# The first right factor of the hyperbolic layer is made under the decay layer, its first products get other PSUM banks, and the row-end products move behind them

## The chip, the cores and the metric

One core of one Trainium2 chip runs the kernel. The metric is the device time of one launch in microseconds, as a median over repeated executions. One more execution is taken by the hardware profiler; all rows and times of day (us from the start of the span) come from that one.

## What is computed

Four graph layers run one after the other on a node matrix x (4096 x 64) and one dense adjacency matrix adj (4096 x 4096, fp32, symmetric pattern but not symmetric values, all entries at least 0). Every layer ends in `x = layernorm(x + layer(x, adj))`. Cut to what matters here:

```python
# layer 0: Chebyshev filter, K = 4: x, L@x, 2L(L@x)-x, ... each times its weight
# layer 1: gated cell and signed attention over adj
# layer 2, "decay": only the last 100 neighbours of a row count, weight halves per step
support = input @ weight
mask = (adj != 0); rank = cumsum(mask, axis=1); deg = rank[:, -1:]
k = minimum(deg, 100); pos = rank - (deg - k)
w = mask * where(pos > 0, 0.5 ** (k - pos), 0.0)
out = w @ support + bias
# layer 3, "hyperbolic": all pairs of nodes
w = adj / adj.sum(axis=1)
log_ij = logmap(x[:, None, :], x[None, :, :])          # mobius_add, norm, arctanh for every pair
agg = einsum('ij,ijc->ic', w, log_ij)
out = expmap(0, agg @ weight + bias)
```

## The kernel before, in words

The nodes are cut into 32 blocks of 128 (NB), eight groups of four blocks (NG, GB = 4, so a group is 512 nodes, GW). The program is written with a tile framework: it allots SBUF and PSUM from pools that open and close as scopes, orders the instructions of each engine by its own priorities, and sets the semaphores. Where `in_order(...)` stands around an instruction, that instruction keeps the written order against the others so marked. PSUM has eight banks of 128 x 512 fp32, and pools take them from bank 0 upwards in the order in which they are opened.

**Layer 2 (lines 1399 to 1512).** The groups are done in two turns, first groups 4 to 7, then 0 to 3. In a turn the loop goes over 64 half blocks h from the last to the first. For each, TensorE adds the masks to the counts (`cnt_ps`, L1450: four products with the constant `follow` into two banks), ScalarE turns the first bank into weights (`wt`, L1455), and VectorE the second (L1457), or ScalarE both while there are seam steps to do (`busy`). One block later TensorE gathers with these weights into four banks `acc_ps` (L1410, L1422). At the end of a turn `copies` (L1479, VectorE) takes the four banks to SBUF as `decayed[g]`.

What follows on a turn is cut into small steps in the list `seam`, of which the loop does one per block: `ends(two)` (L1343) takes two groups through the row-end products with the weight `wd` (`summed`, L1360, eight products, and L1364 on VectorE), the layernorm and the preparation for layer 3 (`turn_prepared`, L1288: transposes into `tr_c` and `tr_o`). The seam of turn 0 is done under turn 1, and the seam of turn 1 under the beginning of layer 3. At the very beginning of layer 2 the seam holds the end of layer 1's last group: edge products (L937, L944), a tanh with a table load (L953), and so on; there ScalarE also copies the last two banks of layer 1 (L1462, L1463), after which these banks go to `acc_ps`.

The pools of layer 2 are opened in the order `ps_c2` (counts: banks 0 and 1), `ps_p2` (two `post` banks: 2 and 3), and then `ps_a2` (the four `acc_ps`: 4 to 7).

**Layer 3 (from line 1514).** It opens `ps_v3` (two buffers of two banks: 0 to 3), `ps_a3` (4 and 5) and `ps_p3` (`post`, 6 and 7). The pairs of nodes are a triangle of 36 tiles of 512 x 512 (`tiles`), rows in the order 4, 5, 6, 7, 0, 1, 2, 3 (`seq`); each is done in two units, n = 0 to 71. A unit n goes through

- `product(n)` (L1577, fp32, four passes of TensorE) of `tr_c` with the right factor of the row, `rights[i][0]`,
- `square(n)` (L1586, ScalarE), then `opposite(n)` (L1596, TensorE, bf16, onto the same banks) with the second right factor,
- `less_one(n)` (L1604, VectorE), a logarithm and two exponentials on ScalarE (L1801, L1802, L1828), the sum with the products (L1826, VectorE), which gives the banks of `product(n)` back to `product(n + 2)`, one more logarithm (L1837),
- `f` (L1811) and `at_d` (L1814) on VectorE, then, a unit later, `gather` (L1638, L1650) on TensorE, and `turn` (L1622 and L1624) for the mirrored half of the tile.

`right(i)` (L1525) makes the right factors of a row: four fp32 and four bf16 products into two `post` banks (L1531) and two copies on ScalarE (L1534) to `rv` and `ro`. For the first row it is called just ahead of `product(0)`; for the others three tiles before they are needed. What a row gathers lies in the two halves of a bank `sums_ps`: partitions 0 to 63 take `at_d`, 64 to 127 take `at_m`. The mirrored sums of a column are kept from row to row in the lower half of `tb`, and for each tile off the diagonal below the first row they are put back by one product with a part of the identity, L1646. That product reads all 128 partitions of `tb`, so its upper half is filled with zeros at the start of the layer (L1544, seven memsets on VectorE).

The beginning of layer 3 is written so:

```python
rights[seq[0]] = right(seq[0])
product(0)
square(0)
less_one(0)
opposite(0)
product(1)
```

Of the kernel before, what the change touches and what calls it, by code (L numbers as in the profile page):

```python
# [28 lines left out]
V_FLOOR = 2.0**-21  # L29
# [33 lines left out]
def gnn4_kernel(  # L63
# [813 lines left out]


    turns_of = [list(range(NG - QG, NG)), list(range(NG - QG))]

    def load2(to, groups, c):

# [456 lines left out]


    decayed = {}

    def ends(two):  # L1343

        bs = slice(two[0] * GB, (two[1] + 1) * GB)
        x2 = nat_a[:, bs, 0:F]
        small = {
            name: sm.tile([P, 2 * GB], F32, name=name) for name in ("ln_ve", "ln_s", "ln_r")
        }
        ve, s, r = small["ln_ve"], small["ln_s"], small["ln_r"]  # L1350
        mv = sm.tile([P, 2 * GB, 2], F32, name="ln_mv")

        def over_all(t):
            return t.unsqueeze(2).to_broadcast([P, 2 * GB, F])

        def summed(ps_p):
            o = ps_p.tile([P, GB, 2 * F], F32, name="post", tag="post")
            for b in range(GB):
                for q, g in enumerate(two):
                    nc.tensor.matmul(  # L1360
                        o[:, b, q * F : (q + 1) * F], lhsT=decayed[g][:, cols(b)], rhs=wd, start=True, stop=True
                    )
            halves = "p (q b) f -> p q b f"
            nc.vector.tensor_tensor(  # L1364
                x2.rearrange(halves, q=2), o.rearrange("p b (q f) -> p q b f", q=2),
                nat_b[:, bs, :].rearrange(halves, q=2), ALU.add,
            )
            st = sm.tile([P, 2 * GB, 6], F32, name="ln_st")
            for b in range(2 * GB):
                nc.vector.bn_stats(st[:, b, :], x2[:, b, :])  # L1370
                nc.vector.bn_aggr(mv[:, b, :], st[:, b, :])
            nc.vector.tensor_scalar_add(ve, mv[:, :, 1], LN_EPS)

        def roots(ps_p):
            nc.scalar.activation(s, ve, AF.Ln)
            nc.scalar.activation(s, s, AF.Exp, scale=0.5)

        def rest(ps_p):

            nc.vector.reciprocal(r, s)  # L1380
            nc.vector.tensor_tensor(r, ve, r, ALU.mult)
            nc.vector.tensor_tensor(s, s, r, ALU.add)
            nc.vector.reciprocal(r, s)
            nc.vector.tensor_scalar_mul(r, r, 2.0)
            nc.vector.tensor_tensor(x2, x2, over_all(mv[:, :, 0]), ALU.subtract)
            nc.vector.tensor_tensor(x2, x2, over_all(r), ALU.mult)

            nc.vector.scalar_tensor_tensor(s, mv[:, :, 1], float(F), r, ALU.mult, ALU.mult)
            nc.vector.tensor_tensor(n2[:, bs], s, r, ALU.mult)

            nc.vector.tensor_reduce(ve, x2, AX.X, ALU.add)
            nc.vector.tensor_scalar_mul(ve, ve, 1.0 / F)
            nc.vector.tensor_tensor(x2, x2, over_all(ve), ALU.subtract)

        return [summed, roots, rest, lambda ps_p: prepare(two)] + [
            lambda ps_p, g=g: turn_prepared(ps_p, g) for g in two
        ]

    with tc.tile_pool(name="mask2", bufs=3) as mk_p, tc.tile_pool(name="wt2", bufs=3) as wt_p, tc.tile_pool(
        name="ps_c2", bufs=1, space=PSUM  # L1400
    ) as ps_c, tc.tile_pool(name="ps_p2", bufs=2, space=PSUM) as ps_p, ExitStack() as ps_a_open:

        def masks2():
            return [mk_p.tile([P, CB, GW], MASK, name=f"m{n}") for n in range(2 * QG)]
# [26 lines left out]
        for turn, groups in enumerate(turns_of):  # L1431
# [9 lines left out]
            for h in reversed(range(2 * NB)):  # L1441
# [31 lines left out]

                gathers += lo + two if jb == 0 else two + lo
                if jb == 0:
                    def copies(ps_p, acc=acc, groups=groups):
                        for q, g in enumerate(groups):
                            decayed[g] = three.tile([P, GW], F32, name=f"sums{q}")
                            nc.vector.tensor_copy(decayed[g], acc[q])  # L1479

                    assert turn == 0 or not seam
                    seam += [lambda ps_p: None, copies]
                    for a in range(2):
                        seam += ends((groups[2 * a], groups[2 * a + 1]))
                busy = bool(seam)
                if seam:
                    seam.pop(0)(ps_p)
# [18 lines left out]

    with tc.tile_pool(name="o3", bufs=1) as op, tc.tile_pool(name="cols3", bufs=3) as cols_p, tc.tile_pool(
        name="w3", bufs=4  # L1510
    ) as wp3, tc.tile_pool(name="el3", bufs=3) as el, tc.tile_pool(name="f3", bufs=2) as fp, tc.tile_pool(
        name="r3", bufs=2
    ) as rp, tc.tile_pool(name="ps_v3", bufs=2, space=PSUM) as ps_v, tc.tile_pool(
        name="ps_a3", bufs=2, space=PSUM
    ) as ps_a, tc.tile_pool(name="ps_p3", bufs=2, space=PSUM) as ps_p:
        HB = CB // 2

        tb = op.tile([P, N], F32, name="tb")
# [1 line left out]
        spread_w = two_w[:, F : 2 * F]  # L1520
        kappa = op.tile([P, 2, NB], F32, name="kappa")

        rvs = [op.tile([P, GW], F32, name=f"rv{q}") for q in range(2)]
        ros = [op.tile([P, GW], BF16, name=f"ro{q}") for q in range(2)]

        def right(i):
            q = seq.index(i) % 2
            for to, w, t in ((rvs[q], to_right, tr_c), (ros[q], to_other, tr_o)):
                ps = ps_p.tile([P, GW], F32, name="post", tag="post")
                for b in range(GB):  # L1530
                    nc.tensor.matmul(  # L1531
                        ps[:, cols(b)], lhsT=w[:, b % 2, :], rhs=t[:, (i * GB + b) // 2, :], start=True, stop=True
                    )
                nc.scalar.copy(to, ps)  # L1534
            return rvs[q], ros[q]


        seq = turns_of[0] + turns_of[1]
        tiles = [(i, j) for n, i in enumerate(seq) for j in seq[n:]]
        NT = len(tiles)  # L1540
        own, mirrored = {}, {}
        nc.gpsimd.memset(tb[F:P, gcols(seq[0])], 0.0)
        for g in seq[1:]:
            nc.vector.memset(tb[0:F, gcols(g)], 0.0)  # L1544

        def load_own(t):
            if t < NT and t not in own:
# [12 lines left out]
            i, j = tiles[n // 2]  # L1560
            return slice(2 * P if i == j and n % 2 else 0, GW)

        rights, sums, fs = {}, {}, {}
        vs, ws, rts = {}, {}, {}
        NU = 2 * NT

        def product(n):

            if n >= NU:
                return  # L1570
            i, j = tiles[n // 2]
            vs[n] = ps_v.tile([P, HB, GW], F32, name="v_ps")
            cs = columns(n)
            for k in range(HB):
                jb = j * CB + (n % 2) * HB + k
                half = slice(jb % 2 * F, jb % 2 * F + F)
                in_order(nc.tensor.matmul(  # L1577
                    vs[n][:, k, cs], lhsT=tr_c[half, jb // 2, :], rhs=rights[i][0][half, cs], start=True, stop=True
                ))

        def square(n):
            if n >= NU:
# [5 lines left out]
        def opposite(n):  # L1588
            if n >= NU:
                return  # L1590
            i, j = tiles[n // 2]
            cs = columns(n)
            for k in range(HB):
                jb = j * CB + (n % 2) * HB + k
                half = slice(jb % 2 * F, jb % 2 * F + F)
                in_order(nc.tensor.matmul(  # L1596
                    vs[n][:, k, cs], lhsT=tr_o[half, jb // 2, :], rhs=rights[i][1][half, cs],
                    start=False, stop=True, skip_group_check=True,
                ))

        def less_one(n):
            if n < NU:
                w = ws[n][:, :, columns(n)]
                nc.vector.tensor_scalar(w, w, -SCALE * SCALE, V_FLOOR * (V_FLOOR + 2.0) * SCALE**2, ALU.add, ALU.max)  # L1604

        def turn(n):

# [19 lines left out]
        def gather(t, h, tm):  # L1627
# [8 lines left out]
            for k in (HB * h, HB * h + 1):  # L1636
                if t is not None:
                    in_order(nc.tensor.matmul(  # L1638
                        bank[0:F, :], lhsT=nat_c[:, j * CB + k, :], rhs=own[t][:, k, :],
                        start=(i == j and k == 0), stop=(j == seq[-1] and k == CB - 1), skip_group_check=True,  # L1640
                    ))
                if tm is not None:
                    above, below = tiles[tm]
                    if k == 0 and above != seq[0]:

                        in_order(nc.tensor.matmul(  # L1646
                            bank[F:P, :], lhsT=ident[:, F:P], rhs=tb[:, gcols(below)],
                            start=True, stop=False, skip_group_check=True,
                        ))
                    in_order(nc.tensor.matmul(  # L1650
                        bank[F:P, :], lhsT=nat_c[:, above * GB + k, :], rhs=mirrored[tm][:, k, :],
                        start=(k == 0 and above == seq[0]), stop=(k == CB - 1), skip_group_check=True,
                    ))
# [125 lines left out]
        for t in range(3):  # L1779
            load_own(t)  # L1780
            load_mirrored(t)
        rights[seq[0]] = right(seq[0])
        product(0)
        square(0)
        less_one(0)
        opposite(0)
        product(1)
        n = 0
        while n < NU + 2 or turns or gathers:
            if n % 2:  # L1790
# [51 lines left out]
                    seam.pop(0)(ps_p)  # L1842
            if n + 6 < NU and tiles[(n + 6) // 2][0] not in rights:
                i = tiles[(n + 6) // 2][0]
                rights[i] = right(i)
            n += 1

        before, last = seam[:-6], seam[-5:]
# [49 lines left out]
```

## Time and profile before

| what | us |
|---|---|
| median of three executions (1404.11, 1404.13, 1407.46) | 1404.13 |
| the profiled execution | 1408.86 |
| its span, first to last instruction | 1407.1 |
| layer 2, from the first counts to the last gather | 762.8 to 964.2 |
| layer 3 and the end of layer 2, from there on | 964.2 to 1407.1 |
| TensorE busy over the span | 1310.2 (93%) |
| VectorE busy | 1052.1 (75%) |
| ScalarE busy | 805.7 (57%) |

A row of the timeline has the start, the duration, the engine (PE is TensorE's multiplication, PEld its weight load, DVE VectorE, ACT ScalarE, POOL GpSimd), the line, the operation, what it writes and reads with its tile shape, and in brackets the idle time of the engine just before it and what ended that. An fp32 product is two passes in the rows. A row of the table by stages has the busy time of each engine in a stretch, and behind them the granted clock of TensorE (1.00 is full), the share of the DMA engines and GB/s.

### The profile page before, as it was taken

The page shows a single profiled execution, that of the slowest core. Times are in us where ns is not written, and L with a number is a line of the kernel's source. Part 1 is how long each engine was busy: PE and PEld are TensorE (multiplying, and loading weights), DVE is VectorE, ACT ScalarE, POOL GpSimd, SP SyncE. Part 2 cuts the span into 40 slices and gives each one's busy share as a digit, 9 for nine tenths or more (in the row PEclk, how much of TensorE's full clock was granted, in tenths as well). Part 3 has the DMA queues.
Part 4 walks back from the last instruction along what each step waited for, and adds up shares of the span by engine and source line. Part 5 has one row for each costly group of instructions (what it writes and reads, how often), then busy time and mean ns, then how long its engine had stood idle before and what let it go on. Part 6 is the DMA issues. An engine that isn't in the chain of part 4 may idle for free.

```text
span 1407.1 us, 19039 instructions
## 1 busy us (share of the span) xinstructions
PE 1310.2 (93%) x6790; PEld 611.1 (43%) x6790; DVE 1052.1 (75%) x2015; ACT 805.7 (57%) x1341; POOL 110.5 (8%) x191
## 2 busy tenths in 40 slices
PE   7999999999999999999999999997889898989893
PEld 5655556556544334444444323333333333333341
DVE  7599889999434257788885224356999999999997
ACT  4544434434000115654424675744989999999894
POOL 2111111011123000010111000000000000000000
PEclk9999999999999999999999999997999999999998
DMA  9999999999799999999985755534244354445330
GB/s 317 392 390 412 376 410 400 405 404 384 290 381 372 388 419 373 421 350 340 329 306 179 239 173 165 181 120 180 78 162 187 149 229 158 184 154 198 138 120 12
DMA packets 108191, 382.16 MB, mean 272 GB/s; under 512 B 20276, under 2 KB 20280, under 8 KB 76472
## 3 DMA queue, kind: packets, MB, share of 16 engines
q1 hardware_dynamic: 87096, 296.17, 57.0%
q0 software_dynamic: 12736, 76.29, 13.2%
q10 hardware_dynamic: 8256, 8.39, 1.7%
q8 instruction: 56, 0.92, 0.3%
q14 instruction: 47, 0.39, 0.1%
HBM read 294.05 MB, written 85.20 MB: 270 GB/s over the span
## 4 chain that ended last, share of the span: by engine, by line
PE 59%; ACT 15%; DVE 15%; DMA 6%; issue 3%; SPq 1%; ACTq 0%; POOL 0%; DVEq 0%
PE pass L566 7%; PE tp L723 6%; PE w_ps L566 6%; PE pass L559 4%; PE cnt_ps L1450 4%; PE a_last L1181 4%; PE a_ps L1181 4%; PE acc_ps L1410 3%; DMA raw<-in_adj_dram 3%; PE h_ps L559 3%; ACT w L1801 2%; ACT rt L1802 2%; DVE rt L1826 2%; ACT w L1586 2%; DVE at_m L1624 2%
## 5 line engine op out<-in xcount | busy, mean ns | idle before, releaser
L730 ACT COPY at<-tp 128x512 f32<-128x512 f32 x248 | 128.5, 598 | 124.2 <-issue 88.6
L1455 ACT ACTIVATE wt<-cnt_ps 128x512 uint16<-128x512 f32 x210 | 116.5, 595 | 65.3 <-PE cnt_ps L1450 63.0
L758 DVE TENSOR_REDUCE dpart<-raw 128x4 f32<-128x2048 f32 x64 | 145.4, 2274 | 4.8 <-DMA raw<-in_adj_dram 4.7
L1638 PE MATMUL sums_ps<-at_d,some 128*64 128x512 f32 x288 | 144.3, 621 | 2.7 <-DVE at_d L1617 1.7
L760 DVE TENSOR_REDUCE lows<-raw 128x1 f32<-128x2048 f32 x64 | 145.4, 2272 | 0.0
L723 PE MATMUL tp<-ident,raw 128*128 128x128 f32 x1024 | 134.4, 285 | 9.8 <-DMA raw<-in_adj_dram 8.3
L723 PEld LDWEIGHTS tp<-ident,raw 128*128 128x128 f32 x1024 | 117.8, 146 | 46.8 <-issue 37.3
L1650 PE MATMUL sums_ps<-at_m,some 128*64 128x512 f32 x224 | 110.0, 613 | 0.0
L1577 PE MATMUL v_ps<-rv,tr_a 64*128 64x512 f32 (+1 forms) x288 | 82.6, 652 | 21.1 <-DVE rt L1826 20.8
L566 PE MATMUL pass<-at,cheb_n 128*128 128x512 f32 x224 | 97.5, 593 | 0.5 <-DVE cheb_n L792 0.5
L566 PE MATMUL w_ps<-at,cheb_n 128*128 128x512 f32 x200 | 91.8, 602 | 0.0
L1826 DVE SCALAR_TENSOR_TENSOR rt<-v_ps,rt 128x1024 f32<-128x1024 f32 x72 | 83.2, 1156 | 5.3 <-ACT rt L1802 4.7
L1450 PE MATMUL cnt_ps<-m,follow 128*64 128x512 fp8e4 x480 | 81.7, 391 | 4.6 <-ACT wt L1455 1.5
L1814 DVE TENSOR_TENSOR at_d<-at_d,f 128x1024 f32<-128x1024 f32 x72 | 83.2, 1156 | 0.1
L1811 DVE SCALAR_TENSOR_TENSOR f<-rt,w 128x1024 f32<-128x1024 f32 x72 | 83.1, 1158 | 0.2 <-ACT rt L1837 0.2
L1624 DVE TENSOR_TENSOR at_m<-post,at_m 128x512 f32<-128x512 f32 x112 | 74.9, 680 | 8.6 <-PE post L1622 8.4
L1837 ACT ACTIVATE rt<-rt 128x1024 f32<-128x1024 f32 x72 | 72.1, 1005 | 11.4 <-DVE rt L1826 10.8
L1457 DVE TENSOR_SCALAR wt<-cnt_ps 128x512 uint16<-128x512 f32 x46 | 31.8, 692 | 59.0 <-PE cnt_ps L1450 59.0
L1801 ACT ACTIVATE w<-w 128x1024 f32<-128x1024 f32 x72 | 72.0, 1000 | 6.5 <-DVE w L1604 6.4
L1622 PE MATMUL post<-ident,f 128*128 128x128 f32 x448 | 68.9, 284 | 4.8 <-DVE at_m L1624 4.5
L1828 ACT ACTIVATE w<-w 128x1024 f32<-128x1024 f32 x72 | 72.4, 1006 | 0.6
L1802 ACT ACTIVATE rt<-w 128x1024 f32<-128x1024 f32 x72 | 72.4, 1005 | 0.6
(426 smaller groups left out, 2279.7 us busy)
## 6 DMA issues: line engine op xcount, KB each, us to landing
at<-adj_t SPq DMA_DIRECT2D x119, 1024.0 KB, 8.5
raw<-in_adj_dram SPq DMA_DIRECT2D x64, 1024.0 KB, 13.3
adj_t<-at POOLq DMA_DIRECT2D x62, 1024.0 KB, 8.2
at_d<-adj_t SPq DMA_DIRECT2D x36, 1024.0 KB, 4.6
at_m<-adj_t SPq DMA_DIRECT2D x28, 1024.0 KB, 6.7
m<-mask_t SPq DMA_DIRECT2D x120, 128.0 KB, 2.9
m<-mask_t SPq DMA_DIRECT2D x60, 256.0 KB, 4.2
mask_t<-mask ACTq DMA_DIRECT2D x28, 256.0 KB, 7.5
```

The source lines that it names most:

```text
L566: in_order(nc.tensor.matmul(ps, lhsT=cheb_n[:, jb, k : k + 2, :], rhs=rhs, start=first, stop=last))
L723: in_order(nc.tensor.transpose(tp[:, cols(b)], raw[:, b, cols(k)], ident))
L730: nc.scalar.copy(at[:, k, :], tp)
L758: in_order(nc.vector.tensor_reduce(dpart[:, g, c, :], raw, AX.X, ALU.add))
L760: in_order(nc.vector.tensor_reduce(lows[:, n : n + 1], raw.rearrange("p b j -> p (b j)"), AX.X, ALU.min))
L1181: in_order(nc.tensor.matmul(ps[q * F : (q + 1) * F, :], lhsT=nat_a[:, c * CB + k, 0:F], rhs=of[q if signed else 0][:, k, :], start=(c == 0 ...
L1450: in_order(nc.tensor.matmul(cnt[a][r * HP : (r + 1) * HP, :], lhsT=follow, rhs=chunks[c][odd][2 * a + r][:, k, :], start=(h == 2 * NB - 1) ...
L1455: in_order(nc.scalar.activation(wt[odd][a], cnt[a], AF.Relu, scale=-128.0))
L1624: work.append(lambda to=to, tp=tp: nc.vector.tensor_tensor(to, tp, to, ALU.mult))
L1638: in_order(nc.tensor.matmul(bank[0:F, :], lhsT=nat_c[:, j * CB + k, :], rhs=own[t][:, k, :], start=(i == j and k == 0), stop=(j == seq[-1] ...
L1650: in_order(nc.tensor.matmul(bank[F:P, :], lhsT=nat_c[:, above * GB + k, :], rhs=mirrored[tm][:, k, :], start=(k == 0 and above == seq[0]), ...
L1826: nc.vector.scalar_tensor_tensor(rt, vs[n][:, :, cs], (1.0 + V_FLOOR) * SCALE, rt, ALU.max, ALU.add)
```

## The change

- `right` is moved up into layer 2. For the first row it becomes the last step of turn 0's seam, so it is done under turn 1. The factors no longer have tiles of their own: the two `rv` lie in an unused quarter of `some`, the first `ro` in `wq_signed`, which layer 1 has left; the second `ro` stays a tile.
- `ps_p2` is opened ahead of `ps_c2`, and `ps_p3` ahead of `ps_v3` and `ps_a3`. So `post` gets banks 0 and 1 in both layers, the counts 2 and 3, and in layer 3 the first product buffer gets 2 and 3, the second 4 and 5, and `sums_ps` 6 and 7.
- Of the four copies at the end of turn 1 two go to ScalarE.
- `product(1)` is written ahead of `less_one(0)` and `opposite(0)`, and from the first product on `behind` chains instructions by ordering them without a semaphore: on TensorE products 0 and 1, `opposite(0)` and then the row-end products, on VectorE `less_one(0)` and then the first sum of the row ends.
- L1646 reads the lower 64 partitions of `tb` alone, with a 64 x 64 part of the identity; the memsets of the upper half go.

```diff
+    rights, begun = {}, {}
+    rvs = [some[:, N // 4 + q * GW : N // 4 + (q + 1) * GW] for q in range(2)]
+    ros = [wq_signed.rearrange("p q h -> p (q h)")[:, 0 : GW // 2].bitcast(BF16)]
+
+    def behind(engine, ins):
+
+        if engine in begun:
+            tc.add_manual_dep(
+                ins.ins, begun[engine],
+                mybir.DependencyInfo(mybir.DependencyClass.NoSync, mybir.DependencyReason.DATA),
+                reason="behind",
+            )
+        begun[engine] = ins.ins.name
...
     with tc.tile_pool(name="mask2", bufs=3) as mk_p, tc.tile_pool(name="wt2", bufs=3) as wt_p, tc.tile_pool(
-        name="ps_c2", bufs=1, space=PSUM
-    ) as ps_c, tc.tile_pool(name="ps_p2", bufs=2, space=PSUM) as ps_p, ExitStack() as ps_a_open:
+        name="ps_p2", bufs=2, space=PSUM
+    ) as ps_p, tc.tile_pool(name="ps_c2", bufs=1, space=PSUM) as ps_c, ExitStack() as ps_a_open:
...
-                    def copies(ps_p, acc=acc, groups=groups):
+                    def copies(ps_p, acc=acc, groups=groups, turn=turn):
                         for q, g in enumerate(groups):
                             decayed[g] = three.tile([P, GW], F32, name=f"sums{q}")
-                            nc.vector.tensor_copy(decayed[g], acc[q])
+                            copy = nc.scalar.copy if turn and q > 1 else nc.vector.tensor_copy
+                            copy(decayed[g], acc[q])
...
                         seam += ends((groups[2 * a], groups[2 * a + 1]))
+                    if turn == 0:
+                        seam.append(lambda ps_p: right(ps_p, seq[0]))
...
-    with tc.tile_pool(name="o3", bufs=1) as op, tc.tile_pool(name="cols3", bufs=3) as cols_p, tc.tile_pool(
+    with tc.tile_pool(name="ps_p3", bufs=2, space=PSUM) as ps_p, tc.tile_pool(name="o3", bufs=1) as op, tc.tile_pool(name="cols3", bufs=3) as cols_p, tc.tile_pool(
...
-        for g in seq[1:]:
-            nc.vector.memset(tb[0:F, gcols(g)], 0.0)
...
-                            bank[F:P, :], lhsT=ident[:, F:P], rhs=tb[:, gcols(below)],
+                            bank[F:P, :], lhsT=ident[F:P, F:P], rhs=tb[F:P, gcols(below)],
...
-        rights[seq[0]] = right(seq[0])
         product(0)
         square(0)
+        product(1)
         less_one(0)
         opposite(0)
-        product(1)
```

More of the change, by code (lines that the diff above doesn't have):

```diff
@@ L879, in gnn4_kernel @@
     turns_of = [list(range(NG - QG, NG)), list(range(NG - QG))]
+    seq = turns_of[0] + turns_of[1]
     def load2(to, groups, c):
@@ L1341, in gnn4_kernel, with right @@
     decayed = {}
+    rights, begun = {}, {}
+    rvs = [some[:, N // 4 + q * GW : N // 4 + (q + 1) * GW] for q in range(2)]
+    ros = [wq_signed.rearrange("p q h -> p (q h)")[:, 0 : GW // 2].bitcast(BF16)]
+    def right(ps_p, i):
+        q = seq.index(i) % 2
+        for to, w, t in ((rvs[q], to_right, tr_c), (ros[q], to_other, tr_o)):
+            ps = ps_p.tile([P, GW], F32, name="post", tag="post")
+            for b in range(GB):
+                nc.tensor.matmul(
+                    ps[:, cols(b)], lhsT=w[:, b % 2, :], rhs=t[:, (i * GB + b) // 2, :], start=True, stop=True
+                )
+            nc.scalar.copy(to, ps)
+        rights[i] = rvs[q], ros[q]
+    def behind(engine, ins):
[4 more added lines that the diff above has]
+                reason="behind",
+            )
+        begun[engine] = ins.ins.name
     def ends(two):
@@ L1359, in summed @@
                 for q, g in enumerate(two):
-                    nc.tensor.matmul(
+                    ins = nc.tensor.matmul(
                         o[:, b, q * F : (q + 1) * F], lhsT=decayed[g][:, cols(b)], rhs=wd, start=True, stop=True
                     )
+                    if begun:
+                        behind("PE", ins)
             halves = "p (q b) f -> p q b f"
-            nc.vector.tensor_tensor(
+            ins = nc.vector.tensor_tensor(
                 x2.rearrange(halves, q=2), o.rearrange("p b (q f) -> p q b f", q=2),
@@ L1367, in summed @@
             )
+            if begun:
+                behind("DVE", ins)
             st = sm.tile([P, 2 * GB, 6], F32, name="ln_st")
@@ L1514, in gnn4_kernel @@
         name="ps_a3", bufs=2, space=PSUM
-    ) as ps_a, tc.tile_pool(name="ps_p3", bufs=2, space=PSUM) as ps_p:
+    ) as ps_a:
         HB = CB // 2
@@ L1521, in gnn4_kernel @@
         kappa = op.tile([P, 2, NB], F32, name="kappa")
[L1523 to L1538, printed above, removed]
         tiles = [(i, j) for n, i in enumerate(seq) for j in seq[n:]]
@@ L1561, in columns @@
             return slice(2 * P if i == j and n % 2 else 0, GW)
-        rights, sums, fs = {}, {}, {}
+        sums, fs = {}, {}
+        ros.append(op.tile([P, GW], BF16, name="ro1"))
         vs, ws, rts = {}, {}, {}
@@ L1576, in product @@
                 half = slice(jb % 2 * F, jb % 2 * F + F)
-                in_order(nc.tensor.matmul(
+                ins = nc.tensor.matmul(
                     vs[n][:, k, cs], lhsT=tr_c[half, jb // 2, :], rhs=rights[i][0][half, cs], start=True, stop=True
-                ))
+                )
+                in_order(ins)
+                if n < 2:
+                    behind("PE", ins)
         def square(n):
@@ L1595, in opposite @@
                 half = slice(jb % 2 * F, jb % 2 * F + F)
-                in_order(nc.tensor.matmul(
+                ins = nc.tensor.matmul(
                     vs[n][:, k, cs], lhsT=tr_o[half, jb // 2, :], rhs=rights[i][1][half, cs],
                     start=False, stop=True, skip_group_check=True,
-                ))
+                )
+                in_order(ins)
+                if n < 1:
+                    behind("PE", ins)
         def less_one(n):
@@ L1603, in less_one @@
                 w = ws[n][:, :, columns(n)]
-                nc.vector.tensor_scalar(w, w, -SCALE * SCALE, V_FLOOR * (V_FLOOR + 2.0) * SCALE**2, ALU.add, ALU.max)
+                ins = nc.vector.tensor_scalar(
+                    w, w, -SCALE * SCALE, V_FLOOR * (V_FLOOR + 2.0) * SCALE**2, ALU.add, ALU.max
+                )
+                if n < 1:
+                    behind("DVE", ins)
         def turn(n):
@@ L1844, in gnn4_kernel @@
                 i = tiles[(n + 6) // 2][0]
-                rights[i] = right(i)
+                right(ps_p, i)
             n += 1
```

## The prediction

> **What bounds the kernel now.** I read the page's sums first, then the table by stages, the chain of waits from 900 to 1010 us, and the timeline row by row at the three places that the edits touch.
>
> ```profile
> PE 1310.2 (93%) x6790; PEld 611.1 (43%) x6790; DVE 1052.1 (75%) x2015; ACT 805.7 (57%) x1341; POOL 110.5 (8%) x191
> ```
>
> TensorE leads, but the sum mixes stages. The table (stretch, length, then PE, PEld, DVE, ACT, POOL; granted clock; DMA share; GB/s) separates them:
>
> ```profile
> 900.00:925.00 25.00, 24.75 (x218) 8.15 (x215) 9.77 (x26) 15.20 (x29) 0.62 (x2) 1.00 0.54 171
> 964.00:975.00 11.00, 8.31 (x40) 6.06 (x39) 6.79 (x14) 2.10 (x3) 0.52 (x1) 0.66 0.89 362
> 975.00:990.00 15.00, 9.17 (x27) 2.62 (x23) 14.53 (x49) 13.53 (x18) 0.00 (x0) 0.50 0.38 156
> 990.00:1010.00 20.00, 18.97 (x80) 7.96 (x80) 19.30 (x40) 19.09 (x22) 0.80 (x2) 0.96 0.28 105
> 1100.00:1200.00 100.00, 90.59 (x429) 36.59 (x428) 96.41 (x155) 96.29 (x132) 1.56 (x2) 1.00 0.45 171
> ```
>
> In layer 2 (first row) TensorE has no gap: each microsecond added there is paid. At the seam (second row) nobody is full, so a chain of waits decides. From 975 VectorE is the bound (14.53 of 15, 19.30 of 20), and later VectorE and ScalarE (96 of 100) with TensorE at 90.6. The seam's chain, by rows of the timeline:
>
> ```profile
> 963.97 2.48 DVE L1479 COPY sums<-acc_ps 128x512 f32<-128x512 f32 x4 [1.24 <-PE acc_ps L1410]
> 966.51 1.16 PE L1531 MATMUL post<-tr_a,to_right 128*128 128x128 f32 x8 [2.36 <-DVE sums L1479]
> 967.75 0.59 ACT L1534 COPY rv<-post 128x512 f32<-128x512 f32 x1 [5.27 <-PE post L1531]
> 968.39 2.08 PE L1577 MATMUL v_ps<-rv,tr_a 64*128 64x512 f32 x4 [0.33 <-ACT rv L1534]
> 970.39 3.67 PE L1360 MATMUL post<-wd,sums 128*128 128x64 f32 x16
> 970.56 1.02 ACT L1586 ACTIVATE w<-v_ps 128x1024 f32<-128x1024 f32 x1 [1.74 <-PE v_ps L1577]
> ...
> 974.10 0.69 DVE L1364 TENSOR_TENSOR nat_a<-post,tr_a 128x512 f32<-128x512 f32 x1 [3.83 <-PE post L1360]
> 974.71 0.68 DVE L1604 TENSOR_SCALAR w<-w 128x1024 f32<-128x1024 f32 x1
> ```
>
> Four copies, right factors, their copy, product(0), row ends, and only then VectorE's run from 974.10. The granted clock is 1.00 up to 967, 0.79 in 967 to 968 and 0.50 until about 991.7, so the row ends take 3.67 us here; the same 16 passes took 2.00 at 893.21 and at 1000.00.
>
> **Part 1: `right` under the decay layer.** It now stands between a gather and a count at about 913, where TensorE has no gap. Its passes at full clock are the rows of a later row: 8 fp32 in 1.13 (1034.51 to 1035.64) and 4 bf16 in 0.32 (1036.71 to 1037.03), 1.45 us. The loop gets one more step with `busy` set; such a step of layer 2 took 2.89 us against 2.72, +0.17 at most. Its two copies (0.59 each) join ScalarE's queue, with both weight pieces of that block behind them and TensorE behind those; ScalarE has 10 us idle in 25, so I take nothing, at worst 0.33. Sum **+1.6** (1.45 to 1.95). It issues no DMA. The seven memsets (L1544) that go took 3.73 us at 966.50, all inside VectorE's 3.83 us wait ahead of 974.10, so their going is worth 0.
>
> **Part 2: the beginning of layer 2.** The built order shows a move that the diff does not: with `ps_p2` in the counts' old banks, ScalarE does weights 1, copy `last_p`, weights 2, the table load (1.28), both tanh (0.28 each), copy `last_a`, and only then weights 3 and 4. Before, both copies stood ahead, and the second tanh came behind weights 3 and 4:
>
> ```profile
> 763.27 1.09 ACT L1455 ACTIVATE wt<-cnt_ps 128x512 uint16<-128x512 f32 x2
> 764.24 0.59 ACT L1463 COPY last_a<-a_last 128x512 f32<-128x512 f32 x1
> 764.71 1.12 ACT L1455 ACTIVATE wt<-cnt_ps 128x512 uint16<-128x512 f32 x2
> 765.84 1.28 ACT L953 ACT_TABLE_LOAD   x1
> 767.14 0.28 ACT L953 ACTIVATE rz<-post 128x128 f32<-128x128 f32 x1
> ```
>
> The second tanh needs the second set of edge products, which ends at 767.8 (L944, 767.30 + 0.49). Then tanh to 768.1, `last_a` to 768.65, two weights to 769.7: the third counts, at 767.73 today, come at about 769.65, and the first gather (behind `last_a`, which frees its banks) at 770.5 instead of 768.28: +2.2. A later wait of TensorE for a mask transfer (0.60 at 779.54) swallows part, since the transfer does not move. **+1.6** (0 if a second such wait does the same, 2.2 if none).
>
> **Part 3: entry of layer 3.** The counts' banks have had their last reader before the last gather. But in the built program the first matmul of product(0) waits for all four `sums` copies: the new pools wait for the old ones as a whole. The copies, two on each engine, end near 963.97 + 2 x 0.62 = 965.3 instead of 966.45. Product(0) then starts at about 965.35 (968.39 today), at full clock lasts 1.13 (L1577, 1035.64), Square 1.02 from 966.55, product(1) beside it, opposite(0) at 967.6, row ends at about 968.0, and L1364's successor at 968.0 + 2.00 + 0.3 = 970.3 with full clock, 971.75 if the clock halves near 967.8 as it does today. `less_one(0)` and `(1)` are done in the wait ahead of it; today they stand in VectorE's full run (974.71 to 975.31 and 977.00 to 977.35, 0.95 us). VectorE carries the bound from there (idle 0.47 of 15 and 0.70 of 20), so its lead is the layer's: 974.10 - 970.3 + 0.95 = 4.75, or 974.10 - 971.75 + 0.95 = 3.3. In the last 3.4 us ahead of the drop TensorE would be busy some 70% (38% today); one stretch of 63% elsewhere was followed by a drop and one was not. I take **-3.8** (-3.3 to -4.8). SP's and POOL's queues keep their order; one early load of adjacency (L1550) waits some 0.4 us longer and is not read until 977.
>
> The Trainium skill speaks on that clock: the page "TensorE: Matmul & The Clock Gate" ties it to TensorE's activity over a window of time; by it a busier seam would keep 1.00, and part 3 would be worth its 4.75 end.
>
> **Part 4: L1646 on 64 rows.** Today its passes cost nothing, because each lies in time on a pass of another product of the same shape:
>
> ```profile
> 1102.58 0.64 PE L1638 MATMUL sums_ps<-at_d,some 128*64 128x512 f32 x1
> 1102.58 0.64 PE L1646 MATMUL sums_ps<-tb,ident 128*64 128x512 f32 x1
> ```
>
> Afterwards its tile is 64*64 next to a 128*64. No row shows such a pair at one time. If it still overlaps: 0. If it stands alone, two passes of 0.47 (L1650 at 1116.49, 1.88 for four) are 0.94 us, and a change of shape costs about 0.1 more (counts to gather, 769.25 to 769.80: 0.55 for 0.43 of streaming). 21 tiles have one: 21 x 0.94 = 19.7, with changes up to 24. TensorE's idle in layer 3 is 9.4 of 100 us, 1.1 per tile of 11.6, so it may all be swallowed; about half is my estimate, +10. Different halves of rows and columns are in use in layer 2's gathers (four 64*64 at once), which is nearest to overlap: I take 0 and keep +10 as a rival.
>
> The Trainium skill is against this edit: "TensorEngine Tiling (Array Packing)", section "Key Properties", says that a change of the tiling mode, not of the tile alone, drains TensorE. By that rule each of the 21 would stand alone, and the sum would be the rival's.
>
> **Sum.** 1.6 + 1.6 - 3.8 + 0 = -0.6 on the profiled execution: 1408.86 to about 1408.3. That execution is 4.7 above the median; microseconds carry over, so 1404.13 becomes **1403.5**. With the bounds of parts 1 to 3 (+1.45 to +4.15, -3.3 to -4.8) the likeliest case runs from 1400.8 to 1405.
>
> **Rivals.**
> - *The pair breaks (slower).* Mechanism, place and price as in part 4: 1403.5 + 10, about 1413 (1404 to 1427). It decides from 0.2 us lost per tile (21 x 0.2 = 4.2, which is 0.3%, about what a measurement can tell from no change). For it: no row of two shapes at once. Against it: TensorE is not the first bound in layer 3. 0.33.
> - *The banks are free early after all.* Product(0) at about 964.2, right after the last gather, 1.15 us sooner: 1402.3. Against it stands the built order's wait for all four copies. 0.10.
> - *The costs hide, the gain does not (faster).* The late weights of part 2 are made up for at mask waits (0), the copies of part 1 cost nothing (+1.45), and the clock stays full (-4.75), with 1 to 2 us more because TensorE is then at full clock through VectorE's run: about 1399.5. For it: TensorE at 0.50 from 975 to 990 was busy only 9.17 of 15, so little hangs on it, which also speaks against. 0.17.
>
> **Numbers.** Forecast 0.40, the others 0.33, 0.10, 0.17. Within 0.3%: 0.40 + 0.10 = 0.50. The range, 1398 to 1416, takes in the third rival but its tail and the first up to a bit above its middle; some 0.2 lies outside, most of it above.
>
> **What would show it.** Part 1: a block near 913 longer by 1.6. Part 2: the third counts at 769.6, and the last gather ending near 967.3 (964.15 today). Part 3, counted from that end: product(0) 1.2 later, and L1364's successor 6.2 to 7.6 after it (9.95 today). Part 4: rows of 64*64 beside at_d with one start, or starts 0.5 apart. Wrong I would be above all if the tiles of the later layer grow from 11.6, or if the last gather ends at 965 or at 970.

## The result, and the profile after

The changed kernel takes 1421.35 us (median of four executions, 1416.48 to 1423.67) against 1404.12 before: 1.0118 times as long, 95% interval 1.0082 to 1.0153. That is 17.2 us slower; 1403.5 was forecast. Its profiled execution took 1423.67 with a span of 1421.9.

First the page's sums, now of the changed kernel:

```profile
PE 1330.0 (94%) x6790; PEld 608.6 (43%) x6790; DVE 1047.0 (74%) x2004; ACT 808.8 (57%) x1345; POOL 110.3 (8%) x191
```

As many TensorE passes as before (6790), but 19.8 us more of TensorE busy time. VectorE was busy 5.1 us less, and the time did not fall with it. The table by stages says where the TensorE time went in (same columns as before):

```profile
1100.00:1200.00 100.00, 93.30 (x403) 34.71 (x402) 91.15 (x148) 91.44 (x122) 1.56 (x2) 1.00 0.46 170
1200.00:1300.00 100.00, 94.43 (x431) 37.56 (x431) 91.09 (x135) 94.22 (x132) 3.13 (x4) 1.00 0.45 168
```

In the steady part of the hyperbolic layer VectorE fell from 96 of 100 to 91, ScalarE from 96 to 91 and 94, and TensorE rose from 90.6 to 93.3 and 94.4, at full clock. The bound has moved towards TensorE. The chain of waits from 1100 to 1300 us, summed by line, says it more sharply. Before, it was ScalarE's chain of logarithms and exponentials:

```profile
by line: ACT rt L1802 11.2%; ACT w L1586 10.8%; ACT w L1801 10.6%; ACT rt L1837 10.2%; ACT w L1828 8.7%; DVE at_m L1624 6.2%; DVE rt L1826 6.0%; DVE at_d L1814 5.1%; DVE f L1811 4.7%; issue 4.5%; PE sums_ps L1638 4.2%; PE v_ps L1577 2.5%; A
```

In the changed kernel the gathers lead, and L1671, the product on 64 rows (L1646 before), carries 5.5%, where it had one pass of 0.57 us on the chain before:

```profile
by line: PE sums_ps L1675 10.2%; PE sums_ps L1663 9.3%; PE v_ps L1592 8.4%; DVE rt L1850 7.9%; DVE at_m L1649 6.7%; PE sums_ps L1671 5.5%; ACT rt L1861 5.4%; ACT w L1604 5.2%; PE post L1647 4.9%; ACT w L1825 4.7%; DVE at_d L1838 4.5%; ACT r
```

The timeline at one tile shows why. A tile shape such as 64*64 is rows x columns: the partitions that a product reads, and those that it writes. First TensorE's rows before, behind the pair at 1102.58 that the prediction shows (L1638 is at_d, L1646 tb, L1650 at_m):

```profile
1103.06 0.59 PE L1638 MATMUL sums_ps<-at_d,some 128*64 128x512 f32 x1
1103.06 0.59 PE L1646 MATMUL sums_ps<-tb,ident 128*64 128x512 f32 x1
1103.49 0.59 PE L1638 MATMUL sums_ps<-at_d,some 128*64 128x512 f32 x1
1103.49 0.59 PE L1650 MATMUL sums_ps<-at_m,some 128*64 128x512 f32 x1
1103.91 0.59 PE L1638 MATMUL sums_ps<-at_d,some 128*64 128x512 f32 x1
1103.92 1.45 PE L1650 MATMUL sums_ps<-at_m,some 128*64 128x512 f32 x3
```

And in the changed kernel (L1663 is at_d, L1671 tb, L1675 at_m):

```profile
1101.15 1.07 PE L1663 MATMUL sums_ps<-at_d,some 128*64 128x512 f32 x2
...
1102.15 1.07 PE L1671 MATMUL sums_ps<-tb,ident 64*64 64x512 f32 x2
...
1103.15 0.64 PE L1675 MATMUL sums_ps<-at_m,some 128*64 128x512 f32 x1
...
1103.16 0.64 PE L1663 MATMUL sums_ps<-at_d,some 128*64 128x512 f32 x1
```

Before, each pass of the tb product started with a pass of at_d. Now two passes of at_d run alone for 1.00 us, then the two 64*64 passes alone for 1.00 us, and only then do at_d and at_m share their time again (1103.15 and 1103.16). Before, the five products took the time of three: tb beside the first at_d, at_m beside the second, and the second at_m alone. Now they take the time of four.

The entry of the layer came out as computed. The last gather ends at 963.21; the rows are those that answer to the chain shown of before:

```profile
963.03 1.29 DVE L1509 COPY sums<-acc_ps 128x512 f32<-128x512 f32 x2 [1.24 <-PE acc_ps L1439]
963.24 1.07 ACT L1509 COPY sums<-acc_ps 128x512 f32<-128x512 f32 x2 [1.71 <-PE acc_ps L1439]
...
964.46 1.56 PE L1592 MATMUL v_ps<-some,tr_a 64*128 64x512 f32 x8 [1.25 <-DVE two_w L1709]
...
967.66 1.77 PE L1385 MATMUL post<-wd,sums 128*128 128x64 f32 x14
...
969.47 0.69 DVE L1391 TENSOR_TENSOR nat_a<-post,tr_a 128x512 f32<-128x512 f32 x1 [1.70 <-PE post L1385]
```

Product(0) starts 1.25 us after the last gather (4.24 before), the row ends run at full clock (14 passes in 1.77), and the first sum on VectorE starts 6.26 us after the last gather (9.95 before).

The beginning of the decay layer, ScalarE's rows; the copy `last_a` (L1492) and the weights behind it stand after both tanh (L954), as the built order said:

```profile
758.72 1.28 ACT L954 ACT_TABLE_LOAD   x1
760.68 0.28 ACT L954 ACTIVATE rz<-post 128x128 f32<-128x128 f32 x1 [0.69 <-PE post L945]
762.18 0.28 ACT L954 ACTIVATE rz<-post 128x128 f32<-128x128 f32 x1 [1.22 <-PE post L945]
762.35 0.58 ACT L1492 COPY last_a<-a_last 128x512 f32<-128x512 f32 x1
762.82 2.43 ACT L1484 ACTIVATE wt<-cnt_ps 128x512 uint16<-128x512 f32 x4
```

The table for the same place (clock in the third column from the right) has something that was not foreseen: after TensorE's wait (2.57 busy of 4) the clock was halved for 3.4 us.

```profile
760.00:764.00 4.00, 2.57 (x14) 1.51 (x13) 0.93 (x6) 2.10 (x6) 0.00 (x0) 0.99 0.39 119
764.00:767.50 3.50, 3.50 (x18) 0.88 (x21) 0.00 (x0) 1.58 (x3) 0.00 (x0) 0.53 0.77 228
```

The span falls into three stretches by two marks in each trace, the first counts and the end of the last gather. The table has them for every kernel of this study (us, one profiled execution each; the medians stand with the experiments):

| kernel | up to the first counts | from there to the last gather | from there to the end |
|---|---|---|---|
| before | 762.77 | 201.38 | 442.95 |
| changed | 756.62 | 206.60 | 458.68 |
| e1_rows128 | 756.30 | 206.58 | 438.82 |
| e2_before64 | 755.75 | 201.41 | 461.84 |
| e3_rows128_pool2 | 756.15 | 203.12 | 438.83 |
| e5_before_pool2 | 755.37 | 203.58 | 443.45 |
| e6_before_64only | 757.67 | 201.37 | 459.56 |
| e7_before_no_tb | 755.84 | 201.38 | 442.68 |
| e8_half_atd | 757.49 | 204.56 | 448.65 |
| e9_right_last | 757.53 | 201.39 | 440.88 |
| e11_pool_memset | 756.96 | 201.40 | 438.54 |
| e12_v_first | 755.07 | 201.39 | 442.74 |

The first stretch does the same work in all of them. The profiled execution of before was 5 to 8 us longer there than the others, which is why its span and the changed kernel's differ by only 14.8. Why it was longer is open: its granted clock was 0.97 over the first 200 us, but that of e5_before_pool2 was too, and it has one of the shortest first stretches. So the stretches are compared, not the spans: +5.2 in the decay layer and +15.7 behind it.

In the decay layer the seven executions that begin in the old order, without `right` under it and without a half-clock stretch, agree within 0.04 us. The last stretch is less firm: time at half clock is spread unevenly over it, 37 us in the changed kernel's and 24 in e1_rows128's (the last 15 us left out), so their difference of 19.9 isn't the price of the product alone.

### The profile page after: what moved, and what is told of

It reads as the page before. It is cut to its first block, busy times and chain, and to the rows that moved or that the text cites. A ratio compares the mean times of both kernels' runs of the same rounds, so it can differ in the third digit from the quotient of the medians.

```text
span 1421.9 us, 19034 instructions
## 1 busy us (share of the span) xinstructions
PE 1330.0 (94%) x6790; PEld 608.6 (43%) x6790; DVE 1047.0 (74%) x2004; ACT 808.8 (57%) x1345; POOL 110.3 (8%) x191
## 4 chain that ended last, share of the span: by engine, by line
PE 65%; DVE 15%; ACT 11%; DMA 5%; issue 3%; ACTq 0%; DVEq 0%; SPq 0%
PE pass L566 7%; PE tp L723 6%; PE w_ps L566 5%; DMA raw<-in_adj_dram 4%; PE cnt_ps L1479 4%; PE a_ps L1182 4%; PE pass L559 4%; PE acc_ps L1439 4%; PE a_last L1182 4%; PE h_ps L559 3%; PE sums_ps L1663 3%; PE p_ps L1173 2%; DVE rt L1850 2%; ACT wt L1484 2%; PE sums_ps L1675 2%
## 5 line engine op out<-in xcount | busy, mean ns | idle before, releaser
L730 ACT COPY at<-tp 128x512 f32<-128x512 f32 x248 | 127.8, 598 | 119.3 <-issue 94.4
L1663 PE MATMUL sums_ps<-at_d,some 128*64 128x512 f32 x288 | 153.3, 642 | 2.3 <-DVE at_d L1642 1.4
L723 PE MATMUL tp<-ident,raw 128*128 128x128 f32 x1024 | 130.9, 281 | 8.5 <-DMA raw<-in_adj_dram 6.7
L723 PEld LDWEIGHTS tp<-ident,raw 128*128 128x128 f32 x1024 | 114.4, 143 | 46.3 <-issue 35.6
L1675 PE MATMUL sums_ps<-at_m,some 128*64 128x512 f32 x224 | 112.5, 624 | 0.0
L1592 PE MATMUL v_ps<-some,tr_a 64*128 64x512 f32 (+1 forms) x288 | 80.3, 636 | 21.7 <-DVE rt L1850 20.5
L1647 PE MATMUL post<-ident,f 128*128 128x128 f32 x448 | 68.9, 286 | 4.8 <-DVE at_m L1649 4.6
```

The lines of the kernel that those rows point to most:

```text
L723: in_order(nc.tensor.transpose(tp[:, cols(b)], raw[:, b, cols(k)], ident))
L730: nc.scalar.copy(at[:, k, :], tp)
L1663: in_order(nc.tensor.matmul(bank[0:F, :], lhsT=nat_c[:, j * CB + k, :], rhs=own[t][:, k, :], start=(i == j and k == 0), stop=(j == seq[-1] ...
L1675: in_order(nc.tensor.matmul(bank[F:P, :], lhsT=nat_c[:, above * GB + k, :], rhs=mirrored[tm][:, k, :], start=(k == 0 and above == seq[0]), ...
```

## The experiments

Two theories went in. **A**: the product on 64 rows no longer shares time with at_d; that is the loss. **B**: the later layer suffers from the entry's new order, other banks or a lower clock.

**e1_rows128**: the changed kernel with the product on 128 rows again.

```diff
-  lhsT=ident[F:P, F:P], rhs=tb[F:P, gcols(below)],
+  lhsT=ident[:, F:P], rhs=tb[:, gcols(below)],
+  for g in seq[1:]:
+      nc.vector.memset(tb[0:F, gcols(g)], 0.0)
```

> The changed kernel with one edit undone: L1671 reads 128 rows of tb again, and the seven memsets are back. Theory A (the 64-row product no longer shares time with at_d): its 42 passes lie on at_d passes again, and of 21 x 1.1 = 23 us of TensorE the 13 to 17 that showed come back: 1404 to 1408, rows of 128*64 with a common start. Rival B (the later layer grew because of the entry's new order, other banks or lower clocks): 1418 to 1421 stays.

Measured: 1403.21, 0.9994 of before (0.9982 to 1.0006), 18 us below the changed kernel. Its passes lie in pairs again (L1665 at_d, L1673 the tb product):

```profile
1097.91 0.64 PE L1665 MATMUL sums_ps<-at_d,some 128*64 128x512 f32 x1
1097.91 0.64 PE L1673 MATMUL sums_ps<-tb,ident 128*64 128x512 f32 x1
1098.39 0.59 PE L1665 MATMUL sums_ps<-at_d,some 128*64 128x512 f32 x1
```

All other edits together make no difference that can be measured. B as the cause of the loss is out.

**e2_before64**: the reverse, the kernel before with that edit alone.

> The kernel before with that edit alone: 64 rows, no memsets. Theory A: 1404 + 15 to 20 = 1419 to 1424, with rows of 64*64 that start when at_d's passes have ended. Rival B: 1404, within 2.

Measured: 1419.84, 1.0114 (1.0097 to 1.013), as theory A had it.

**e3_rows128_pool2**: e1_rows128 with the decay layer's pools in the old order.

```diff
-  name="ps_p2", bufs=2, space=PSUM ... name="ps_c2", bufs=1, space=PSUM
+  name="ps_c2", bufs=1, space=PSUM ... name="ps_p2", bufs=2, space=PSUM
```

> As e1_rows128, and the decay layer's pools are opened in the old order. Theory A2 (the new order of ScalarE's queue at the start of that layer costs 2.4 us, and the half clock after TensorE's wait there 1.1 more): 3.5 below e1_rows128, at 1401 to 1404, and no stretch at half clock near 764. Rival C (the half clock there is chance, and the later queue is caught up at mask waits): within 1 of e1_rows128.

Measured: 1402.02, 0.9992 (0.9979 to 1.0006). The times put it 1.2 below e1_rows128, too little to tell the two apart; the traces do: the first gather comes 5.52 us after the first counts (7.72 in e1_rows128, 5.51 before), and the decay layer is 3.46 shorter. What remains against before, 203.12 - 201.38 = 1.74, is the moved `right`.

**e5_before_pool2**: the kernel before with only that pool order changed.

> The kernel before with only the decay layer's pools in the new order. Theory A2: 1404 + 3.5 = 1407.6, first gather 2.4 later after the first counts, then a stretch at half clock. Rival C: 1404 to 1405.

Measured: 1406.0, 1.0016 (1.0001 to 1.0031), 2.5 us. The first gather is 2.19 later after the first counts and the decay layer 2.20 longer, but no half clock followed. So the queue's order costs 2.2 in the traces, and the half clock (1.3 of the changed kernel's 5.2) is not tied to it: e8_half_atd, whose layer begins in the old order, has a stretch at half clock there (0.50 from 762 to 766). Theory A2 is right in its first term, C in its second.

**e6_before_64only**: e2_before64 with the memsets kept; every engine's order is that of before, and only the shape of 21 products differs.

> The kernel before with L1646 on 64 rows and the memsets kept, so that only the shape of 21 products differs. Theory A (the shape alone takes them out of at_d's time): as e2_before64, 1418 to 1421. Rival E (the missing memsets let later work fall worse, and that is part of the 16): 1408 to 1415.

Measured: 1420.01, 1.0119 (1.0097 to 1.0142). The shape alone makes the whole loss, 16.5 us; leaving out the memsets makes no difference that can be measured.

**e7_before_no_tb**: the kernel before without the product.

```diff
-  if k == 0 and above != seq[0]:
-      in_order(nc.tensor.matmul(bank[F:P, :], lhsT=ident[:, F:P], rhs=tb[:, gcols(below)], ...))
```

> The kernel before without L1646: the mirrored sums of the earlier rows are left out of the output. It takes two slots of 0.47 us from each of 21 tiles, 19.7 us of TensorE. Theory A (before, VectorE and ScalarE bound that layer, and only the 64-row form made TensorE the bound): 1399 to 1403. Rival F (TensorE bounds it already, and each 0.94 counts in full): 1384 to 1390.

Measured: 1402.34, 0.9991 (0.9975 to 1.0006): no difference from before that can be measured. Without the tb product each at_m (L1644 here) stands beside an at_d, and four products take the time of two:

```profile
1096.80 0.64 PE L1638 MATMUL sums_ps<-at_d,some 128*64 128x512 f32 x1
1096.81 0.64 PE L1644 MATMUL sums_ps<-at_m,some 128*64 128x512 f32 x1
...
1098.14 0.59 PE L1638 MATMUL sums_ps<-at_d,some 128*64 128x512 f32 x1
1098.14 0.59 PE L1644 MATMUL sums_ps<-at_m,some 128*64 128x512 f32 x1
```

The table, from 200 to 300 us after the last gather, shows TensorE idle more (it was busy 89 to 91 of 100 before) and the others as full as ever:

```profile
1157.22:1257.22 100.00, 84.25 (x413) 35.64 (x414) 97.32 (x159) 97.67 (x146) 2.95 (x4) 1.00 0.45 170
```

The same stretch in e6_before_64only, where the product stands alone:

```profile
1159.04:1259.04 100.00, 92.70 (x413) 36.42 (x412) 91.81 (x146) 92.56 (x135) 3.13 (x4) 1.00 0.41 157
```

The two kernels have the same half-clock stretches up to the end of the first row and are at one time there (the first logarithm of tile 5,5 starts 102.9 and 103.0 us after the last gather). From there on they differ in the tb product: 442.68 - 102.9 = 339.8 and 459.56 - 103.0 = 356.6. That is 16.8 us for 21 products, 0.80 each.

**e8_half_atd**: is it the number of rows, or that two neighbours differ in shape? In e6_before_64only the at_d product just ahead of each tb product is cut to rows 0 to 63 as well.

```diff
+  rows = slice(0, F) if k == 0 and tm is not None and tiles[tm][0] != seq[0] else slice(0, P)
-  bank[0:F, :], lhsT=nat_c[:, j * CB + k, :], rhs=own[t][:, k, :],
+  bank[0:F, :], lhsT=nat_c[rows, j * CB + k, :], rhs=own[t][rows, k, :],
```

> As e6_before_64only, and the at_d product ahead of each of those 21 reads only rows 0 to 63, so that it is 64*64 too (half of that sum is left out). Theory G (what matters is that both have one shape): the two share their time again, 1404 to 1408, rows of 64*64 with a common start. Rival H (a 64-row fp32 product in columns 64 to 127 never shares time): 1418 to 1424.

Measured: 1406.83, 1.0017 (0.9999 to 1.0036), 13 us below e6_before_64only with as many passes. The rows (L1639 at_d, L1647 tb) start together:

```profile
1100.99 0.64 PE L1639 MATMUL sums_ps<-at_d,some 64*64 64x512 f32 x1
1101.00 0.64 PE L1647 MATMUL sums_ps<-tb,ident 64*64 64x512 f32 x1
1101.47 0.59 PE L1639 MATMUL sums_ps<-at_d,some 64*64 64x512 f32 x1
1101.48 0.59 PE L1647 MATMUL sums_ps<-tb,ident 64*64 64x512 f32 x1
...
1102.00 0.64 PE L1651 MATMUL sums_ps<-at_m,some 128*64 128x512 f32 x1
```

Theory G holds, H falls: the 64-row product shares its time as soon as its neighbour has its shape. The two also read different rows here, 0 to 63 and 64 to 127; but the pairs of 128*64 share all their rows, and in the decay layer of before four 64*64 products, two on either half of the rows, start together (L1422 at 769.80 and 769.81). The change of shape itself is cheap: 0.52 us from the last 64*64 pass to at_m's first, where 0.42 to 0.48 stand between passes of one shape.

**e9_right_last**: towards a version that beats both. e3_rows128_pool2, with `right` behind the last gather, under the copies of the sums.

```diff
-  if turn == 0:
-      seam.append(lambda ps_p: right(ps_p, seq[0]))
...
         seam.pop(0)(ps_p)
+        right(ps_p, seq[0])
```

> As e3_rows128_pool2, but the first right factor is made behind the last gather, while the sums are copied, with the old pool order in the decay layer. The decay layer gets its 1.7 us back; product(0) waits for the factor's copy, some 0.7 to 1.0 us longer. Expected 0.7 to 1.0 below e3_rows128_pool2: 1401. Rival: the factor's copy stands behind two copies of sums on ScalarE and all is lost again, 1402 to 1403.

Measured: 1401.05, 0.9977 of before (0.9964 to 0.999). The decay layer is back at 201.39 and product(0) starts 2.24 us after the last gather instead of 1.25, as expected. The times alone, 1.0 apart, can't tell it from e3_rows128_pool2.

**e11_pool_memset**: the same, with the memsets on GpSimd (`nc.gpsimd.memset` in the loop).

> As e9_right_last, with the seven memsets on GpSimd instead of VectorE. In e9_right_last they fill VectorE for 3.73 us right behind its copies and end 0.3 after the first square is there. If they still cost something: 0.3 to 1 below e9_right_last, 1400 to 1401. If VectorE's first sum waits for the row ends anyway: the same as e9_right_last.

Measured: 1401.47, 0.9976 (0.9963 to 0.999); VectorE's first sum starts 7.27 us after the last gather, in e9_right_last 7.26. It waits for the row ends; the memsets cost nothing there either.

**e12_v_first**: the same, with the hyperbolic layer's pools in the old order.

> As e11_pool_memset, with the hyperbolic layer's pools in the old order, so that the first product's banks are those of the old counts. Theory J (a first product waits for whatever had the banks of its whole pool, and not for the layer): it waits for the factor's copy alone, no longer for VectorE's copies of sums, and starts about 1.7 to 1.9 after the last gather instead of 2.24; 0.4 below e11_pool_memset, which the times can hardly tell. Rival K (it waits for the whole of the old layer in any order): 2.2 stays.

Measured: 1401.99, 0.9983 (0.9972 to 0.9994). The start that theory J gave did not come: product(0) still starts 2.24 us after the last gather, and what it waits for is the second factor's copy, which it does not read:

```profile
958.70 1.56 PE L1593 MATMUL v_ps<-some,tr_a 64*128 64x512 f32 x8 [0.94 <-ACT wq_signed L1355]
```

The product's own banks are those of the old counts (0 and 1), so the wait is not for its own banks. But its pool, `ps_v3`, takes banks 0 to 3 in this order, and these hold both `post` banks, out of which that copy reads. So the wait can be for the banks of its whole pool, as J has it, or for the old layer as a whole, as K has it: J's time was wrong, and which of the two holds is open.

e9_right_last, e11_pool_memset and e12_v_first, 2.5 to 3.2 us under before, can't be told apart. They are the only ones that are below both kernels by more than the interval, by 0.2%.

## Why the prediction was wrong, point by point

- **Part 1, `right` under the decay layer: right.** +1.6 was forecast; 1.74 measured (e3_rows128_pool2 against before).
- **Part 2, ScalarE's order at the start of that layer: right in its delay, a little short in its sum.** The first gather was to come 2.2 later and came 2.19 later in e5_before_pool2. Of that, 0.6 was to be swallowed by a later wait for a mask; it was not: the layer is 2.20 longer there. In the changed kernel another 1.3 came on top, behind a half-clock stretch that some traces have and others don't.
- **Part 3, the entry: right.** The first sum was to start 6.2 to 7.6 after the last gather, and starts at 6.26; product(0) 1.2 after, and 1.25 it is. The layer was to lead by 3.8 and leads by 442.95 - 438.82 = 4.1 where the tb product is left as it was (e1_rows128). That size is less firm than the starts: by the medians of e3_rows128_pool2 and before it is 1.45 + 1.74 = 3.2, and e9_right_last, e11_pool_memset and e12_v_first, whose first sums start alike, spread over 4.2 us in this stretch. The memsets were worth nothing that can be measured. The row ends kept full clock, as they should by the page "TensorE: Matmul & The Clock Gate" of the Trainium skill, section "Part 1: The HAM clock gate", which ties the clock to how busy TensorE has just been. The half clock came near 972, when TensorE had been idle since 969.4.
- **Part 4, L1646 on 64 rows: wrong, and the whole error.** The step that failed is the overlap, the term of 0: the 64*64 product was taken to share its time with at_d, and it stood alone, for 16.5 us. The step took 0, "nearest to overlap", because four 64*64 products of the decay layer run at once. That row shows products of *one* shape side by side, and the question was about two. There was a better row, which the same part used only for the price of a change of shape: counts (128*64) and gathers (64*64) in turn, 0.55 us for 0.43 of streaming, one after the other. e8_half_atd against e6_before_64only shows the condition. The reading that the passes "cost nothing" before was not right either: beside at_d they kept an at_m from standing there, and e7_before_no_tb shows the tile one product's time shorter on TensorE without them. The Trainium skill's page "TensorEngine Tiling (Array Packing)", section "Key Properties", has the rule, that a change of the tiling mode drains TensorE; it was quoted and then not followed. This case's rows agree with it: at_d's passes at 1101.15 and the 64*64 passes at 1102.15 stand one after the other, 1.00 us each.
- **The rival's price was too low as well.** It had the right mechanism, but halved 19.7 us to 10, on the reckoning that TensorE's idle time would swallow half. Measured were 16.5 (e6_before_64only), 84% of 19.7. The idle share of 9.4 of 100 was not free room: where the added product stood alone, TensorE got no fuller than 92 to 94 of 100. From 90 it had about 3 us in 100 to give, not 9. The likely reason, which no run tested, is that each unit goes through TensorE, ScalarE and VectorE in turn with two product buffers, and that TensorE works in a written order. On the other side, taking the product out of the kernel before (e7_before_no_tb) gained nothing that can be measured. The same 19.7 us of TensorE were thus worth nothing measurable in one direction and 16.5 in the other: the layer stood near the point where TensorE becomes the bound.
- **The other two rivals.** The banks were not free early (1.25, not near 0). The faster case would have needed part 2 to hide, which it didn't.

Together: +2.2 and +1.7 in the decay layer, -4.1 at the entry, +16.5 from the shape make +16.3; the medians say +17.2. Without the last term it would be -0.2, close to the -0.6 of the forecast.

## What to carry to other kernels

Before a matmul is made smaller, look in the timeline at which product it shares its start with: in this kernel two products in different columns ran at once when they had one shape, and one after the other when one of them was cut from 128 to 64 rows, so that zeros in the unused rows were 16 us cheaper than leaving them out. Idle time of an engine near its limit need not be room: here 84% of the added work was paid, so price it in full unless a run shows that it disappears. And read the built order of the engines when pools are moved, since a pool's place alone moved a copy behind two tanh and cost 2.2 us.

## What the runs showed of the hardware that was not expected

- Stretches at half clock fall differently in executions of code that is the same up to that point. The start of the decay layer had one in the changed kernel, e1_rows128 and e8_half_atd, and none in e5_before_pool2, though TensorE waits there as long as in e1_rows128 (first gather 7.70 and 7.72 us after the first counts). Each moved a stage of a single profiled execution by 1 to 3 us, so a difference of this size between two traces shows an effect only where neither has such a stretch, as in the decay layer of before, e3_rows128_pool2 and e5_before_pool2.
- The cut product's own row did not get longer: a mean of 618 ns a pass on 128 rows and 637 on 64. What it lost is seen only in the start times of its neighbours, not in its mean duration.
